# The first attention's second sequence: rows turned by VectorE and moved by DMA instead of turned by TensorE

## The chip, the cores and the metric

One core of a Trainium2 chip runs the whole kernel. Its engines are TensorE (matrix products, which it writes to PSUM), VectorE, ScalarE and GpSimd (called DVE, ACT and POOL in the profile), and SyncE (SP), which here only issues transfers; sixteen DMA engines carry what SP, ScalarE and GpSimd issue. Every engine works through its own list of instructions in order and waits at semaphores for the others. The metric is the device time of one execution in microseconds, the median of several runs.

## The reference, cut to what matters

Two transformer layers with a layer norm after each part. The change lies in the first part, a linear attention that reads a memory `M`, `z`:

```python
# L0_attn: B, S, HID = 2, 512, 512; H, HKV, D = 32, 8, 128; G = 4
q = (hidden_states @ Wq.T + bq).reshape(b, s, H, D)
sig_q = jax.nn.elu(q) + 1.0
q_sel = sig_q[:, :, ::G, :]                      # 8 heads are read
num = jnp.einsum('bshd,hde->bshe', q_sel, M)
den = jnp.einsum('bshd,hd->bsh', q_sel, z)[..., None] + EPS
retrieved = num / den
out_heads = jnp.repeat(retrieved, G, axis=2)
output = out_heads.reshape(b, s, H * D) @ Wo.T
...
x = _layernorm(x + _L0_attn_ref(x, ...))
x = _layernorm(x + _L0_ffn_ref(x, ...))
x = _layernorm(x + _L1_attn_ref(x, ...))
x = _layernorm(x + _L1_ffn_ref(x, ...))
```

The query product contracts over the 512 hidden columns, so each sequence's rows are needed with the hidden index on the partitions: the input has to be transposed.

## The kernel before

All arithmetic here is in float32. A sequence has 512 rows in four tiles `xs[b][t]` of 128 rows (on partitions) by 512 columns. `xt` is a sequence transposed: hidden index on partitions, four blocks `k` of 128, and 512 row positions in the free dimension. For each of eight heads `queries(b, xt, h)` makes four products into one PSUM tile `pq` (eight PSUM buffers in rotation), ScalarE takes Exp (L388) and Relu (L390) of it with the bias `bq`, and VectorE joins them to `q = min(e, 1) + r` (L392, called elu here). The tiles of `e` and `r` have two buffers, so the Exp of a head waits for the elu of two heads before. The sixteen `q` tiles are kept for the read stage.

The rows of sequence 0 are transposed tile by tile between products (`first_rows`, `first_queries`). Those of sequence 1 are transposed in one go after head 6 of sequence 0, by `transposed(xs[1], "a01")`: sixteen TensorE transposes into four PSUM tiles (L127), two copied out by ScalarE and two by VectorE (L129).

Meanwhile the weights are prepared. `sum_weights(eng, h)` adds up the four groups of `Wo` of a head (L407, L409; heads 1, 2, 4 and 6 on VectorE, 0, 3, 5 and 7 on GpSimd) from the tiles `wo`, a pool of six buffers, two to a head, so that a later head's load waits for an earlier head's sum; the result `wos` has four buffers. `turn_memory` transposes `M`. `fold(h)` multiplies the two (L414) and ScalarE writes the result with its row mean taken off to `mw[:, h, :511]` (L416, L417). The last column of `mw`, index `LAST`, holds `z`, copied by GpSimd at the start (L348). The first two folds come after head 0 of sequence 1, the others between later heads.

Beside that, the first feed-forward's weights are examined: `largest` reduces the first `gu` tile on VectorE, `over_partitions` (L190 to L194) and `scales` (L201 to L205) take the maximum over partitions by way of TensorE, and `check_up` then scales a block of `gu` on ScalarE (L463) and compares it on VectorE (L210). From head 3 of sequence 1 on there are three checks a head.

The read stage follows: for each of eight row tiles `read` multiplies the eight heads' `q` with `mw` (L428), ScalarE copies the denominators (L432) and scales three heads (L441), VectorE adds five (L450) and GpSimd the rest.

The loads are all issued by SP (but one row tile of sequence 0, by ScalarE) in this order: rows of sequence 0 and `wq` mixed, `wq` to the last, rows of sequence 1 (`load_x(1)`), `m`, the sixteen `wo` halves with the first `gu` before the last four, the other `gu`, then the second layer's small weights.

The order on each engine other than GpSimd is made by a planner that follows the program's order and its own estimate of when things are ready; `tc.issue_after(ins)` keeps what is traced inside it behind `ins` on that engine. GpSimd's list is in program order.

A later stage turns rows in another way already: `turn_squares` has VectorE transpose a tile in squares of 32 by 32 (L551), and `move_squares` moves the squares to their places with sixteen DMAs of 64 KB, 128 bytes a piece, on three queues (L292).

Of the kernel before, what the change touches and what calls it, by code (L numbers as in the profile page):

```python
# [10 lines left out]
F32 = mybir.dt.float32  # L11
# [3 lines left out]
AF = mybir.ActivationFunctionType  # L15
ALU = mybir.AluOpType
# [3 lines left out]
P = 128  # L20
B, S, HID = 2, 512, 512
NT = S // P
NK = HID // P
# [6 lines left out]
LAST = HID - 1  # L30
SQ = 32
# [7 lines left out]
def kernel(  # L39
# [19 lines left out]
    nc = tc.nc  # L59
# [6 lines left out]
    xtp = ctx.enter_context(tc.tile_pool(name="xtp", bufs=2))  # L66
# [14 lines left out]
    def psum(name):  # L81
        return ps.tile([P, 512], F32, tag="mm", name=name)


    xs = [[], []]

    def load_x(b, tiles=range(NT)):
        for t in tiles:
            x = xp.tile([P, HID], F32, tag="x", name=f"x_{b}_{t}")
            eng = nc.scalar if b == 0 and t == 1 else nc.sync  # L90
            eng.dma_start(x, x_in[b, ts(t, P), :])
            xs[b].append(x)

    load_x(0, range(2))
    bq = const.tile([D, NH], F32, tag="bq", name="bq")
    z = const.tile([D, NH], F32, tag="z", name="z")
# [18 lines left out]
    copies = []  # L115

    def transposed(rows, name, in_turn=False):

        xt = xtp.tile([P, NK, S], F32, tag="xt", name=f"xt_{name}")
        done = None  # L120
        for k in range(NK):
            pt = psum(f"pt_{name}_{k}")
            with ExitStack() as tied:
                if in_turn and k:
                    tied.enter_context(tc.issue_after(done.ins))
                for t in range(NT):
                    done = nc.tensor.transpose(pt[:, ts(t, P)], rows[t][:, ts(k, P)], ident)  # L127
            move = nc.vector.tensor_copy if k == 1 or k % 2 > in_turn else nc.scalar.copy
            copies.append(move(xt[:, k, :], pt))  # L129
        return xt  # L130
# [47 lines left out]
    def largest(blocks, name):  # L178

        k = len(blocks)  # L180
        mx = small.tile([P, k], F32, tag=f"mx{k}", name=f"mx_{name}", bufs=1)
        for i, w in enumerate(blocks):
            nc.vector.reduce_max(mx[:, i : i + 1], w, AX.X)
        return mx

    def over_partitions(mx, name):

        k = mx.shape[-1]
        pm = psum(f"pmx_{name}")
        nc.tensor.transpose(pm[:k, :P], mx, ident)  # L190
        top = small.tile([k, 1], F32, tag=f"top{k}", name=f"top_{name}", bufs=1)
        nc.vector.reduce_max(top, pm[:k, :P], AX.X)
        dg = small.tile([k, k], F32, tag=f"dg{k}", name=f"dg_{name}", bufs=1)
        nc.vector.tensor_scalar_mul(dg, ident[:k, :k], top)  # L194
        return dg
# [112 lines left out]
    with tc.tile_pool(name="a0w", bufs=1) as a0w, tc.tile_pool(name="a0", bufs=2) as a0:  # L308
        wq = []
        for h in range(NH):  # L310
# [7 lines left out]
            elif h == 1:  # L318
                nc.sync.dma_start(bq, bq_in)
                nc.sync.dma_start(z, z_in)  # L320
        load_x(1)
        m = a0w.tile([D, NH, D], F32, tag="m", name="m")
        nc.sync.dma_start(m, m_in)

# [20 lines left out]


        mw = a0w.tile([D, NH, HID], F32, tag="mw", name="mw")
        nc.gpsimd.tensor_copy(mw[:, :, LAST], z)  # L348

        def query_products(pq, xt, h, at):  # L350
            for k in range(NK):
                done = nc.tensor.matmul(  # L352
                    pq[:, at], wq[h][:, k, :], xt[:, k, at],
                    start=(k == 0), stop=(k == NK - 1),
                )
            return done

        def first_rows(xt, t):

            pt = psum(f"pt_a00_{t}")  # L360
            for k in range(NK):
                done = nc.tensor.transpose(pt[:, ts(k, P)], xs[0][t][:, ts(k, P)], ident)
            pt = pt.rearrange("p (k t) -> p k t", k=NK)
            nc.scalar.copy(xt[:, :2, ts(t, P)], pt[:, :2])
            nc.vector.tensor_copy(xt[:, 2:, ts(t, P)], pt[:, 2:])
            return done

        def first_queries(pq, xt):

            done = first_rows(xt, 0)  # L370
            for t in range(NT):
                if t + 1 < NT:
                    with tc.issue_after(done.ins):
                        done = first_rows(xt, t + 1)
                with tc.issue_after(done.ins):
                    done = query_products(pq, xt, 0, ts(t, P))
            return done

        def queries(b, xt, h):

            pq = psum(f"pq_{b}_{h}")
            if b == h == 0:
                done = first_queries(pq, xt)
            else:
                done = query_products(pq, xt, h, slice(0, S))

            e = a0.tile([D, S], F32, tag="e", name=f"e_{b}_{h}")
            nc.scalar.activation(e, pq, AF.Exp, bias=bq[:, h : h + 1])  # L388
            r = a0.tile([D, S], F32, tag="r", name=f"r_{b}_{h}")
            nc.scalar.activation(r, pq, AF.Relu, bias=bq[:, h : h + 1])  # L390
            q = a0.tile([D, S], F32, tag="q", name=f"q_{b}_{h}", bufs=16)
            nc.vector.scalar_tensor_tensor(q, e, 1.0, r, ALU.min, ALU.add)  # L392
            qs[b].append(q)
            return done

        def turn_memory():

            for i in range(2):
                pt = psum(f"pt_m_{i}")
                for j in range(4):  # L400
                    nc.tensor.transpose(pt[:, ts(j, P)], m[:, 4 * i + j, :], ident)
                nc.scalar.copy(m[:, 4 * i : 4 * i + 4, :].rearrange("d h e -> d (h e)"), pt)

        def sum_weights(eng, h):

            w, w1 = wos[h]
            eng.tensor_add(w, w, w1)  # L407
            s = a0.tile([D, HID], F32, tag="wos", name=f"wos{h}", bufs=4)
            eng.tensor_add(s, w[:, 0, :], w[:, 1, :])  # L409
            wos[h] = s  # L410

        def fold(h):
            p = psum(f"pmw_{h}")
            nc.tensor.matmul(p, m[:, h, :], wos[h], start=True, stop=True)  # L414
            c = small.tile([P, 1], F32, tag="col", name=f"col_{h}", bufs=2)
            nc.scalar.mul(c, p[:, LAST:], -1.0)  # L416
            nc.scalar.activation(mw[:, h, :LAST], p[:, :LAST], AF.Identity, bias=c)  # L417
# [65 lines left out]
        xt = xtp.tile([P, NK, S], F32, tag="xt", name="xt_a00")  # L483
        with tc.issue_after(queries(0, xt, 0).ins):
            queries(0, xt, 1)
        for h in range(2, NH):
            queries(0, xt, h)
            if h == 4:
                sum_weights(nc.gpsimd, 0)
                turn_memory()  # L490
                sum_weights(nc.vector, 1)
            elif h == 6:
                xt1 = transposed(xs[1], "a01")
                sum_weights(nc.vector, 2)
        sum_weights(nc.gpsimd, 3)
        for h in range(NH):
            queries(1, xt1, h)
            if h == 0:
                sum_weights(nc.vector, 4)
                sum_weights(nc.gpsimd, 5)  # L500
                fold(0)
                fold(1)
                with tc.issue_after(copies[-1].ins):
                    mx_up = largest(
                        [gus[0][:, a].rearrange("p k i -> p (k i)") for a in range(2)], "up"
                    )
            elif h == 1:
                top_up = over_partitions(mx_up, "up")
            elif h == 2:
                sc_up, inv_up = scales(top_up, "up")  # L510
                fold(2)
                fold(3)
                sum_weights(nc.vector, 6)
                sum_weights(nc.gpsimd, 7)
            elif h == 3:
                fold(4)
            elif h == 5:
                fold(5)
                fold(6)
            elif h == 6:  # L520
                fold(7)
            if h >= 3:
                for _ in range(3):
                    check_up(*checks.pop(0))
# [64 lines left out]
    xt1 = fp.tile([P, NT, NK, P], F32, tag="it11", name="xt_f01", bufs=1)  # L589
# [289 lines left out]
    for b in range(B):  # L879
# [5 lines left out]
        xt = xt_a1[b]  # L885
# [4 lines left out]
        for j in range(2):  # L890
            p = psum(f"pqk_{b}_{j}")
# [11 lines left out]
        for t in range(NT):  # L903
            p = psum(f"pv_{b}_{t}")
# [167 lines left out]
    t = NT - 1  # L1072
# [248 lines left out]
```

## Time and profile before

| | |
|---|---|
| median of three runs | 470.58 us (470.02 to 470.64) |
| the profiled execution | 470.72 us, span 468.7 us |
| granted TensorE clock, mean | 0.998 |
| TensorE, VectorE, ScalarE, GpSimd busy | 461.0, 329.5, 267.5, 115.1 us |
| query products (L352), 152 instructions | 56.9 us |
| folds and reads: first L428 product | starts at 72.32 us |

A time of the profile's lines counts from the start of the span. Sequence 0's heads run from about 6 to 37 us, sequence 1's to 72, the read stage to about 131; the feed-forward, the second attention and the second feed-forward take the rest, with TensorE busy throughout. A timeline line gives start, duration, engine, line, operation, output and inputs, shapes and count, and in brackets the idle time before it and what ended that. Lines of stretches give the length, the busy time of each engine with its number of instructions, the granted clock, the busy share of the DMA engines and GB/s.

### The profile page before, as it was taken

Reading aid. Unit: us, or ns where it says so; the run is one execution under the profiler, and the core shown is the slowest. Engines: PE = TensorE matmul, PEld = TensorE weight load, DVE = VectorE, ACT = ScalarE, POOL = GpSimd, SP = SyncE. Lnnn points to the kernel's source line nnn. Section 1 sums busy time; section 2 is a strip of 40 time slices with the busy share of each in tenths; the row PEclk is TensorE's granted clock in tenths of the full one; section 3 lists DMA queues with packets and bytes.
Section 4 is the critical chain, followed back from the end, with each engine's and each line's share of the span. In section 5 each row is a group of like instructions: output and inputs, shape, how many; then the busy total and the mean of one; then the engine's idle time right before and its main releaser. Section 6 shows DMA issues by size and latency. Waiting matters only on the chain.

```text
span 468.7 us, 5727 instructions
## 1 busy us (share of the span) xinstructions
PE 461.0 (98%) x1883; PEld 329.0 (70%) x1883; DVE 329.5 (70%) x627; ACT 267.5 (57%) x507; POOL 115.1 (25%) x144
## 2 busy tenths in 40 slices
PE   9999999999999999999999999999999999999994
PEld 8454444434478888888866567888888888888884
DVE  1165677767876767775979889895755778998632
ACT  3344799557756767456756842584645768443101
POOL 0235101566543053600357032000000000050111
PEclk9999999999999999999999999999999999999999
DMA  8989900000006500051390000000000000001001
GB/s 284 381 297 363 387 9 0 0 0 3 1 1 134 201 1 3 11 162 45 91 390 31 0 1 1 1 0 1 1 0 1 0 1 1 1 24 45 37 31 45
DMA packets 21651, 35.02 MB, mean 75 GB/s; under 512 B 9840, under 2 KB 10736, under 8 KB 21616
## 3 DMA queue, kind: packets, MB, share of 16 engines
q1 hardware_dynamic: 19616, 33.73, 20.7%
q10 hardware_dynamic: 1872, 0.56, 0.5%
q8 instruction: 22, 0.36, 0.3%
q0 software_dynamic: 128, 0.26, 0.3%
q14 instruction: 13, 0.11, 0.1%
HBM read 31.40 MB, written 2.10 MB: 71 GB/s over the span
## 4 chain that ended last, share of the span: by engine, by line
PE 71%; ACT 7%; DVE 5%; issue 3%; POOL 0%; POOLq 0%; DVEq 0%; ACTq 0%
PE pm L1111 17%; PE pg_f L611 9%; PE pu_f L611 9%; PE pc L1111 8%; PE pdm L1199 7%; PE pd_f L666 4%; PE pdc L1199 4%; DVE x L450 3%; PE pqk L893 3%; PE po L428 2%; ACT y L441 2%; ACT t L463 2%; PE pv L906 2%; PE pot L989 1%; PE po L1005 1%
## 5 line engine op out<-in xcount | busy, mean ns | idle before, releaser
L428 PE MATMUL po<-mw,q 128*128 128x512 f32 x128 | 57.1, 598 | 0.3 <-DVE mv_a L139 0.2
L352 PE MATMUL pq<-xt_a,wq 128*128 128x512 f32 (+1 forms) x152 | 56.9, 526 | 0.0
L145 POOL TENSOR_TENSOR rstd_f<-mv_f,ln_eps 128x1 f32<-128x1 f32 x15 | 4.4, 293 | 169.3 <-DVE mv_f L1214 130.2
L428 PEld LDWEIGHTS po<-mw,q 128*128 128x128 f32 x128 | 22.9, 189 | 32.1 <-issue 17.7
L352 PEld LDWEIGHTS pq<-xt_a,wq 128*128 128x128 f32 x152 | 26.2, 190 | 27.4 <-issue 25.7
L1111 PE MATMUL pm<-r,ugu 128*128 128x512 f32 x152 | 37.7, 389 | 0.0
L1111 PE MATMUL pm<-r,it_early 128*128 128x512 f32 x144 | 36.7, 392 | 0.0
L1111 PEld LDWEIGHTS pm<-r,ugu 128*128 128x128 f32 x152 | 28.5, 188 | 5.9
L1111 PEld LDWEIGHTS pm<-r,it_early 128*128 128x128 f32 x144 | 27.0, 188 | 6.1 <-issue 0.5
L169 ACT ACTIVATE ta_f<-y_f,below_half 128x512 int8<-128x512 f32 (+1 forms) x22 | 15.9, 721 | 27.0 <-DVE y_f L157 26.7
L450 DVE SCALAR_TENSOR_TENSOR x<-po,den,x 128x511 f32<-128x511 f32 x40 | 29.8, 745 | 1.9
L1121 DVE SCALAR_TENSOR_TENSOR ev_q<-pm,ev_q 128x512 f32<-128x512 f32 x27 | 18.6, 688 | 14.4 <-PE pm L1111 14.4
L637 DVE SCALAR_TENSOR_TENSOR it_f<-tb_f,ta_f 128x512 fp32r<-128x512 int16 (+1 forms) x22 | 15.4, 702 | 18.3 <-ACT tb_f L170 18.3
L445 POOL TENSOR_TENSOR y<-y,y 128x511 f32<-128x511 f32 x16 | 20.3, 1271 | 31.5 <-ACT y L441 30.8
L388 ACT ACTIVATE e<-pq,bq 128x512 f32<-128x512 f32 x16 | 11.1, 692 | 24.1 <-PE pq L352 20.6
L611 PE MATMUL pg_f<-xh,tu 128*128 128x512 f32 x88 | 24.3, 398 | 0.0
L1120 ACT ACTIVATE ev_q<-pc 128x512 f32<-128x512 f32 x27 | 16.0, 593 | 14.2 <-PE pc L1111 14.1
L465 POOL TENSOR_SCALAR td<-wd,inv_down 128x512 fp32r<-128x512 f32 x11 | 18.2, 1668 | 22.1 <-DVE inv_down L205 22.1
L611 PE MATMUL pg_f<-xl,tu 128*128 128x512 f32 x88 | 23.6, 390 | 0.0
L611 PE MATMUL pu_f<-xh,tu 128*128 128x512 f32 x88 | 23.5, 389 | 0.0
L611 PE MATMUL pu_f<-xl,tu 128*128 128x512 f32 x88 | 23.5, 389 | 0.0
L1001 ACT ACTIVATE x<-x,off_f,rstd_f 128x512 f32<-128x512 f32 x7 | 5.7, 816 | 27.7 <-POOL off_f L1000 27.7
(315 smaller groups left out, 1087.5 us busy)
## 6 DMA issues: line engine op xcount, KB each, us to landing
gu<-in_gu SPq DMA_DIRECT2D x20, 512.0 KB, 7.9
wo<-in_wo SPq DMA_DIRECT2D x16, 512.0 KB, 6.9
wd<-in_wd SPq DMA_DIRECT2D x20, 256.0 KB, 4.5
wq<-in_wq SPq DMA_DIRECT2D x8, 256.0 KB, 4.9
x<-in_x SPq DMA_DIRECT2D x7, 256.0 KB, 5.4
out<-x SPq DMA_DIRECT2D x7, 256.0 KB, 2.0
wqkv<-in_wqkv SPq DMA_DIRECT2D x1, 768.0 KB, 10.8
xt_f<-squares SPq DMA_DIRECT2D x9, 64.0 KB, 2.4
```

The lines of the kernel that those rows point to most:

```text
L169: nc.scalar.activation(a[:n], y, AF.Relu, bias=below_half[:n])
L352: done = nc.tensor.matmul(pq[:, at], wq[h][:, k, :], xt[:, k, at], start=(k == 0), stop=(k == NK - 1),)
L428: nc.tensor.matmul(po, qs[b][h0 + j][:, ts(t, P)], mw[:, h0 + j, :], start=True, stop=True,)
L445: nc.gpsimd.tensor_add(ys[0][:, :LAST], ys[0][:, :LAST], y[:, :LAST])
L450: steps.append(nc.vector.scalar_tensor_tensor(x[:, :LAST], four[j][:, :LAST], d, x[:, :LAST], ALU.mult, ALU.add))
L465: eng.tensor_scalar(out, w, factor, None, ALU.mult)
L611: nc.tensor.matmul(pp[a], t[:, a, i % NK, :], x2[b][i], start=(i == 0), stop=(i == 2 * NK - 1),)
L666: nc.tensor.matmul(pd, inter[b][c][:, ts(t, P)], td[c].bitcast(F32R), start=(c == 0), stop=(c == last),)
L1111: nc.tensor.matmul(p, w, x, start=(left[id(p)] == begun[id(p)]), stop=(left[id(p)] == 1))
L1120: nc.scalar.activation(ev, pc, AF.Copy, scale=CROSS)
L1121: nc.vector.scalar_tensor_tensor(ev, pm, MAIN, ev, ALU.mult, ALU.add)
L1199: nc.tensor.matmul(p[:, :w], got[j // 4][1][kind][:, j % 4], down_parts[j][kind][:, cols], start=(j == 0 and kind == kinds[0]), stop=(j == ...
```

## The change

Sequence 1's rows are no longer transposed by TensorE. VectorE transposes each row tile in squares of 32 by 32 into `turned_rows`, a part of `mw` that is not yet in use, so laid out that 128 row positions with the same place in their square lie side by side. Sixteen DMAs on ScalarE's queue then move strips of 32 partitions, in pieces of 512 bytes, to `xt1`: `move_rows(i)` issues four, for row positions `i*128` to `i*128+127`. Two groups of eight are issued, behind the Relu of head 0 and that of head 1. The row positions of `xt1` are in another order than the rows; Exp and Relu of sequence 1 write their results in the right order by a rearranged output (`ordered`).

The loads of sequence 1's rows are issued after `wq2`, ahead of `wq3` to `wq7`. The copy of `z` into the last column of `mw` comes after sequence 1's first head in the program. Three orders are tied anew: the turns behind the last copy of `first_rows`, the third head's sum behind the fourth elu, and the `gu` maximum behind the seventh elu (before: behind the last copy of `transposed`).

```diff
             elif h == 1:
                 nc.sync.dma_start(bq, bq_in)
                 nc.sync.dma_start(z, z_in)
-        load_x(1)
+            elif h == 2:
+                load_x(1)
...
         mw = a0w.tile([D, NH, HID], F32, tag="mw", name="mw")
-        nc.gpsimd.tensor_copy(mw[:, :, LAST], z)
-
...
+        turned_rows = mw[:, :NT, :].rearrange("p a f -> p (a f)")
+        turned_rows = turned_rows.rearrange("p (b t c) -> p b t c", t=NT, c=SQ)
+        xt1 = xtp.tile([P, NK, S], F32, tag="xt", name="xt_a01")
+
+        def turn_rows(t):
+            nc.vector.transpose(
+                turned_rows[:, :, t, :], xs[1][t].rearrange("p (b c) -> p b c", c=SQ)
+            )
+
+        def move_rows(i):
+
+            src = mw[:, :NT, :].rearrange("p a f -> p (a f)")
+            src = src.rearrange("p (k j f) -> p k j f", k=NK, j=P // SQ)
+            for j in range(P // SQ):
+                nc.scalar.dma_start(xt1[ts(j, SQ), :, ts(i, P)], src[ts(i, SQ), :, j, :])
+
...
-            nc.vector.tensor_copy(xt[:, 2:, ts(t, P)], pt[:, 2:])
+            copies.append(nc.vector.tensor_copy(xt[:, 2:, ts(t, P)], pt[:, 2:]))
             return done
...
+        relus, elus = [], []
+
         def queries(b, xt, h):
...
             e = a0.tile([D, S], F32, tag="e", name=f"e_{b}_{h}")
-            nc.scalar.activation(e, pq, AF.Exp, bias=bq[:, h : h + 1])
+
+            if b == 1:
+                pq = pq.rearrange("p (i t c) -> p i t c", t=NT, c=SQ)
+
+            def ordered(u):
+                return u.rearrange("p (t i c) -> p i t c", t=NT, c=SQ) if b == 1 else u
+
+            nc.scalar.activation(ordered(e), pq, AF.Exp, bias=bq[:, h : h + 1])
             r = a0.tile([D, S], F32, tag="r", name=f"r_{b}_{h}")
-            nc.scalar.activation(r, pq, AF.Relu, bias=bq[:, h : h + 1])
+            relus.append(nc.scalar.activation(ordered(r), pq, AF.Relu, bias=bq[:, h : h + 1]))
             q = a0.tile([D, S], F32, tag="q", name=f"q_{b}_{h}", bufs=16)
-            nc.vector.scalar_tensor_tensor(q, e, 1.0, r, ALU.min, ALU.add)
+            elus.append(nc.vector.scalar_tensor_tensor(q, e, 1.0, r, ALU.min, ALU.add))
...
         with tc.issue_after(queries(0, xt, 0).ins):
             queries(0, xt, 1)
+        with tc.issue_after(copies[-1].ins):
+            for t in range(NT):
+                turn_rows(t)
         for h in range(2, NH):
+            with tc.issue_after(relus[h - 2].ins):
+                if h < 4:
+                    for i in range(2):
+                        move_rows(2 * h - 4 + i)
             queries(0, xt, h)
             if h == 4:
                 sum_weights(nc.gpsimd, 0)
                 turn_memory()
                 sum_weights(nc.vector, 1)
             elif h == 6:
-                xt1 = transposed(xs[1], "a01")
-                sum_weights(nc.vector, 2)
+                with tc.issue_after(elus[3].ins):
+                    sum_weights(nc.vector, 2)
         sum_weights(nc.gpsimd, 3)
         for h in range(NH):
             queries(1, xt1, h)
             if h == 0:
+                nc.gpsimd.tensor_copy(mw[:, :, LAST], z)
                 sum_weights(nc.vector, 4)
...
-                with tc.issue_after(copies[-1].ins):
+                with tc.issue_after(elus[6].ins):
                     mx_up = largest(
```

## The prediction

> **What bounds the kernel now.** I read the page first, then the chain of waits, then each engine's timeline over the first 75 us, then the stretch table. The page says TensorE is busy 98% of the span; the stretches show where that holds for the stage of the change:
>
> ```profile
> core 0: us, PE busy (x) PEld busy (x) DVE busy (x) ACT busy (x) POOL busy (x), PEclk, DMA share, GB/s
> 0.00:11.70 11.70, 10.65 (x67) 9.95 (x68) 1.90 (x9) 3.56 (x7) 0.92 (x8) 1.00 0.85 283
> 11.70:23.40 11.70, 11.70 (x29) 5.19 (x28) 1.78 (x3) 4.27 (x7) 2.84 (x2) 1.00 1.00 382
> 23.40:32.00 8.60, 8.60 (x27) 4.20 (x26) 6.00 (x7) 3.49 (x6) 3.27 (x3) 1.00 0.83 266
> 32.00:40.00 8.00, 8.00 (x32) 4.46 (x31) 5.07 (x8) 3.49 (x6) 3.76 (x2) 1.00 0.99 386
> 40.00:51.00 11.00, 11.00 (x29) 4.86 (x28) 4.47 (x9) 5.29 (x10) 3.77 (x2) 1.00 0.98 374
> 51.00:60.00 9.00, 9.00 (x23) 3.98 (x22) 7.36 (x14) 8.38 (x17) 1.45 (x1) 1.00 0.86 320
> 60.00:72.00 12.00, 12.00 (x30) 5.30 (x29) 8.68 (x22) 12.00 (x24) 0.00 (x0) 1.00 0.01 2
> ```
>
> From 11.7 to 51 us TensorE has no gap, at full clock, while ScalarE and VectorE are busy under half of most of these stretches: TensorE sets the pace. The DMA engines are full too (share 0.83 to 1.00), which matters below. From 51 to 72 ScalarE is full beside TensorE. The timeline of TensorE shows the work that the change removes (start, duration, line, tile, count):
>
> ```profile
> 25.32 7.03 PE L352 MATMUL pq<-xt_a,wq 128*128 128x512 f32 x16
> 32.19 1.91 PE L127 MATMUL pt_a<-ident,x 128*128 128x128 f32 x16
> 33.94 7.03 PE L352 MATMUL pq<-xt_a,wq 128*128 128x512 f32 x16
> ```
>
> The products resume at 33.94, so the 16 transposes hold the array for 33.94 - 32.19 = 1.75 us. Of the 7.03 us that follow the first half is head 7 of sequence 0; head 0 of sequence 1 begins at 33.94 + 3.43 = 37.37 (3.43 is the step from one head to the next), the first reader of the turned rows.
>
> **Part by part.** *Removed*: 1.75 us of TensorE, on the path. Also two ScalarE copies (1.07 us at 33.54) and two VectorE copies (2 x 0.68 at 35.11 and 36.31); both engines have idle time there, so nothing. Sum so far -1.75.
>
> *Loads moved on SP's queue.* The four row loads (1 MB) pass five wq loads, wq3 to wq7, and the latter come four issues later. So wq3 takes the place of wq7, issued 8.2 and landed 4.8 us later, at 13.0; head 3 starts at 17.8. Cover 4.8 us, growing by about 2 us a head: nothing. Later loads keep their place. The row loads take the places of wq3 to wq6, the last issued about 7.5 with 4.1 to landing: rows there at 11.6.
>
> *Added on VectorE*: four square transposes. The same instruction on the same shape is in the trace:
>
> ```profile
> 122.08 0.71 DVE L551 STREAM_TRANSPOSE squares<-x 128x512 f32<-128x512 f32 x1
> 141.19 2.10 ACTq L292 DMA_DIRECT2D xt_f<-squares  x3
> ```
>
> 4 x 0.71 = 2.84 us. VectorE is idle 2.25 us before 12.21, 2.74 before 15.64 and 6.67 before 23.00, so they fit; the last ends at 11.6 + 0.71 = 12.3 at best, 13.5 if the first elu (12.21, 0.69) goes ahead. I take 13.
>
> *Added on ScalarE's queue*: 16 issues. Bounds of one: 0.42 us (the row load of 128 pieces on this queue at 0.74) and 0.70 (the three above, 512 pieces each). The new ones have 128 pieces, so I take 0.42: 6.7 us, at most 11.2. Behind them wait the Exp and Relu of heads 1 and 2, and behind those VectorE's elu and two of the eight PSUM buffers. ScalarE's idle time between 12.2 and 32.4 is 12.9 us, and no head's result is read before the read stage at 72: nothing, unless ScalarE falls some 13 us behind (four heads of 3.43 us in the buffers, an estimate). First group 13.0 to 16.4, head 1's Exp and Relu 1.25, second group to 21.0 (25.5 by the upper price).
>
> *When the rows have landed.* The 64 KB moves here took 2.2 to 3.9 us on this queue with no load beside them; loads in the busy stretch took up to 9.5. So 23.2 to 35.0. They are wanted at 37.37 - 1.75 = 35.62. Even the upper end is in time. One rule of the skill speaks against this: "DMA: Bandwidth & Descriptors", section "Rules for kernel authors", calls transfers under 64 KB mostly overhead, and the page's fit in "Anatomy of one DMA", for GpSimd's path, makes 2.15 us of each. One after another that is 34 us, by estimate, and rows at 47: TensorE would wait 11.8 us, 480.8 in all. The trace overlaps them: sixteen such moves, issued from 141.19 on over three queues, had landed by 150.3, 9.1 us.
>
> *The DMA engines carry 1 MB more.* Bounds: 1.05 MB at the 400 GB/s of the best microseconds (16 to 23) is 2.6 us; the 128-byte moves of 141 to 150 took 0.69 x 9 = 6.2. Pieces of 512 bytes lie between; I take 3. Loads behind it (wo, then gu) come so much later, less some 1.5 us of idle share between 23 and 30. Who is late next: VectorE, which stands in order behind a load:
>
> ```profile
> 33.37 1.22 DVE L407 TENSOR_TENSOR wo<-wo,wo 128x1024 f32<-128x1024 f32 x1 [3.97 <-DMA wo<-in_wo]
> ...
> 39.84 1.23 DVE L407 TENSOR_TENSOR wo<-wo,wo 128x1024 f32<-128x1024 f32 x1 [1.45 <-DMA wo<-in_wo]
> 40.98 0.68 DVE L392 SCALAR_TENSOR_TENSOR q<-e,r 128x512 f32<-128x512 f32 x1
> 41.86 0.69 DVE L409 TENSOR_TENSOR wos<-wo 128x512 f32<-128x512 f32 x1 [0.20 <-PE pmw L414]
> 42.47 0.69 DVE L392 SCALAR_TENSOR_TENSOR q<-e,r 128x512 f32<-128x512 f32 x1
> 46.26 0.28 DVE L192 TENSOR_REDUCE top_up<-pmx_up 2x1 f32<-2x128 f32 x1 [3.11 <-PE pmx_up L190]
> ```
>
> If the load at 39.84 is d later, the work behind it ends at 42.9 + d (the small wait for pmw gone), and top_up with dg_up at 43.4 + d. TensorE wants dg_up at 49.59 - 1.75 = 47.84 (pbc_up, L201). So d up to 4.4 costs nothing; by my bounds d is at most 6.2 - 1.5 = 4.7, a wait of 0.3 at most. The first gu load lands at 37.1 + d and feeds pmx_up at 45.95 - 1.75 = 44.2 after a reduce of 1.28: cover 5.8. The second (39.0 + 7.4 = 46.4) is wanted on ScalarE at 54.08 - 1.75: cover 5.9.
>
> *z's column copy* (0.20 us on GpSimd) moves behind the landing of the moves and ahead of a sum that began at 35.97 and whose result goes into a buffer free only at 42.83: nothing. The fold that writes the same tile comes at 42.36: later than the moves.
>
> *Exp and Relu with reordered writes* (16, runs of 32). No row has such runs. The nearest is L364, 256 elements in two runs, 0.372 us against 0.585 for 512 in one: the slope of 0.83 ns leaves 0.16, the whole of a one-column instruction (L416, 0.17), so a break in a run costs at most 0.01 us. 15 breaks x 0.01 x the ten in ScalarE's full stretch (heads 3 to 7) = 1.5 us as the upper end; I take nothing, as the two runs cost nothing.
>
> *Does the gain pass the ScalarE-bound stretch?* That stretch starts on TensorE's word (inv_up at 50.2 after pbc_up), so it starts 1.75 earlier with the same work in it. Sum: 470.72 (the profiled execution, span 468.7) - 1.75 = 468.97; the median of the runs is 0.14 lower: **468.8**.
>
> **Rivals.**
> *1. The two queues share their places in flight (slower).* SP's issues wait for older landings (in the view of waits: who, for what, us in total, times, longest):
>
> ```profile
> SPq L332 <- DMA wo<-in_wo: 5.6, 2, 4.8
> SPq L314 <- DMA x<-in_x: 1.7, 2, 1.4
> ```
>
> and the wq load issued about 6.8 goes out as the row load eight issues before it lands (1.64 + 5.2). If ScalarE's moves draw on the same eight places, the eighth move waits for wo2's last half (issued 15.5, landed 25), the second group goes out 26.3 to 29.7 and the third head's wo load, free to go at 22.8, waits until about 29: 6.2 late, some 8 with the added megabyte. The rows still land before 35.6. But d = 8 is 3.6 over the 4.4 above: TensorE waits 3.6 at L201, net +1.85, **472.4**. It decides from d = 4.4 and turns the sign at 6.2. For it: the waits shown. Against: only SP issues here, so sharing is not seen, and the planner may place VectorE's blocked sum elsewhere.
> *2. The gain is eaten in ScalarE's full stretch (no change).* 12.00 of 12.00 busy from 60 to 72: with reordered writes at their upper end, 1.5 of the 1.75 is lost, **470.3**. Against: the L364 row. A planner's new order of that stretch could do the same.
> *3. Rows late.* If moves and loads share the engines packet by packet, loads of 2 to 4 KB against 512 bytes, the last may land after 37.37. At 41, **474.2**. Against: the 35.0 bound above.
>
> **How the numbers follow.** A difference under 0.2% (0.94 us) can't be told from no change. Forecast 0.54, own range 468.0 to 469.6 (1.75 less up to 0.8 lost, more by up to 0.8 if a shift of VectorE's order also closes small waits in the read stage, where TensorE has 80 products in 35.47 against 34.3 at the head's pace). Rival 2: 0.17, within 0.2%. Rival 1: 0.20, rival 3: 0.09, slower. The range 468.0 to 472.8 takes in rival 1 and leaves out the high end.
>
> **What would show it.** Right: no transposes between heads 6 and 7; the first product of sequence 1 near 35.6 with no gap before it; pbc_up near 47.8; ScalarE's den column at 73.0 in place of 74.79; Exp of sequence 1 at 0.69. Wrong: a gap of TensorE before the first pq of sequence 1 (rival 3); a gap before pbc_up with VectorE held by a wo load, and ScalarE's issues spread out to 25 us or more (rival 1); Exp and Relu above 0.8 us (rival 2).

## The result, and the profile after

The changed kernel takes **472.69 us** (median of 15 runs, 470.67 to 474.13) against 470.64 (470.02 to 471.16) for the kernel before on the same chip: ratio 1.0044, 95% interval 1.0032 to 1.0055. It is slower by 2.05 us, where 1.8 less was forecast. The profiled execution took 473.49 (span 471.7), 2.77 more than the one of before and 0.8 above its own median; the steps below are read from it. Of all executions in this document one, of e8_half, took 795.71 us at a mean granted clock of 0.557; it is left out of that run's figures.

TensorE's timeline first (start, duration, line, tile, count, and in brackets the idle time ahead and what ended it):

```profile
25.13 10.46 PE L351 MATMUL pq<-xt_a,wq 128*128 128x512 f32 x24
38.68 5.12 PE L351 MATMUL pq<-xt_a,wq 128*128 128x512 f32 x8 [3.08 <-ACT m L427]
43.64 1.88 PE L439 MATMUL pmw<-wos,m 128*128 128x512 f32 x4
45.35 3.60 PE L351 MATMUL pq<-xt_a,wq 128*128 128x512 f32 x8
...
52.42 0.38 PE L201 MATMUL pbc_up<-dg_up,ones 2*128 2x2 f32 x2
```

Before, head 1 of sequence 1 began here:

```profile
42.52 3.60 PE L352 MATMUL pq<-xt_a,wq 128*128 128x512 f32 x8
```

The transposes between head 7 of sequence 0 and head 0 of sequence 1 are gone, and sequence 0 ends at 35.59; 35.62 was forecast. But then TensorE stands still for 3.08 us, so that the first head of sequence 1 starts at 38.68 instead of 37.37 before: 1.31 later. The same eight products that take 3.60 one head later take 5.12 here: 1.52 more. Together 2.83, which is 45.35 less the 42.52 at which the next head began before. It is passed on whole: the read stage begins at 75.15 (72.32 before), and the span is 3.0 longer. The stretches show the second term (length, then busy time and instructions of TensorE, its weight loads, VectorE, ScalarE and GpSimd, then granted clock, DMA share and GB/s):

```profile
36.00:37.00 1.00, 0.00 (x0) 0.00 (x0) 0.00 (x0) 1.00 (x3) 0.57 (x1) 1.00 0.87 215
...
38.00:39.00 1.00, 0.32 (x1) 0.35 (x2) 1.00 (x3) 0.65 (x2) 0.42 (x1) 0.60 0.88 307
39.00:40.00 1.00, 1.00 (x2) 0.48 (x2) 1.00 (x2) 0.85 (x2) 0.11 (x1) 0.50 1.01 410
40.00:41.00 1.00, 1.00 (x2) 0.34 (x2) 1.00 (x3) 0.53 (x2) 0.00 (x0) 0.50 0.99 332
41.00:42.00 1.00, 1.00 (x3) 0.39 (x2) 0.99 (x2) 1.00 (x2) 0.00 (x0) 0.70 0.75 225
42.00:43.00 1.00, 1.00 (x4) 0.49 (x3) 0.82 (x2) 1.00 (x3) 0.82 (x1) 1.00 0.83 143
```

After the wait the granted clock is 0.5 to 0.7 for some 3 us. From 36 to 37 TensorE and VectorE are idle, GpSimd for nearly half, and ScalarE is full: it is catching up. Why it is behind shows in its own timeline, with its DMA issues (ACTq):

```profile
12.48 3.15 ACTq L372 DMA_DIRECT2D xt_a<-mw  x3
15.68 0.69 ACT L413 ACTIVATE e<-pq,bq 128x512 f32<-128x512 f32 x1 [3.69 <-DMA wq<-in_wq]
16.27 0.68 ACT L415 ACTIVATE r<-pq,bq 128x512 f32<-128x512 f32 x1
16.93 8.63 ACTq L372 DMA_DIRECT2D xt_a<-mw  x5
25.67 0.69 ACT L413 ACTIVATE e<-pq,bq 128x512 f32<-128x512 f32 x1 [8.72 <-DMA xt_a<-mw]
...
27.00 8.17 ACTq L372 DMA_DIRECT2D xt_a<-mw  x8
35.27 0.69 ACT L413 ACTIVATE e<-pq,bq 128x512 f32<-128x512 f32 x1 [8.33 <-DMA xt_a<-mw]
...
37.56 1.09 ACT L427 COPY m<-pt_m 128x512 f32<-128x512 f32 x2
```

The Exp of head 3 stood here before:

```profile
21.21 0.69 ACT L388 ACTIVATE e<-pq,bq 128x512 f32<-128x512 f32 x1 [2.17 <-PE pq L352]
```

It runs at 35.27 now, 14 us late. One issue takes 0.59 us, so five are 2.95, yet they need 8.63: the rest is waiting for earlier transfers to land. The trace's semaphore records show which. A transfer tells its landing by a semaphore; SP's and ScalarE's transfers take turns on the same eight, and an issue waits until the last user of its semaphore has landed. Of the last eight moves five go out 0.02 us after such a landing (at 27.00, 29.15, 30.83, 33.09 and 34.57); three of the five ahead of them wait in the same way for loads of SP (`m` and two of `wo`). In e1, where GpSimd issues the moves, they use eight others. So the "places in flight" of the prediction are semaphores of this program.

What TensorE waited for at 38.68 is not what the bracket says. The copies of the turned M end at 38.65 (37.56 + 1.09), and the profile puts the wait down to them, because they came last. But the last move, issued at 34.57, landed at 38.33, and that is near too. GpSimd's copy of `z`, which may run only when the moves have read `mw`, began 0.10 us before TensorE:

```profile
38.58 0.53 POOL L531 COPY mw<-z 128x8 f32<-128x8 f32 x1 [2.00 <-DVE wo L432]
```

Two other profiles with the same wait part the two: e12, the changed kernel once more, and e7 (below). First e12, then e7:

```profile
36.80 1.09 ACT L427 COPY m<-pt_m 128x512 f32<-128x512 f32 x2
38.46 0.24 POOL L531 COPY mw<-z 128x8 f32<-128x8 f32 x1 [3.39 <-DMA xt_a<-mw]
38.56 5.20 PE L351 MATMUL pq<-xt_a,wq 128*128 128x512 f32 x8 [3.48 <-ACT e L413]
```

```profile
36.91 1.09 ACT L429 COPY m<-pt_m 128x512 f32<-128x512 f32 x2
37.67 0.27 POOL L533 COPY mw<-z 128x8 f32<-128x8 f32 x1 [1.76 <-DMA xt_a<-mw]
37.77 5.37 PE L353 MATMUL pq<-xt_a,wq 128*128 128x512 f32 x8 [2.50 <-ACT m L429]
```

TensorE starts 0.10 us after the copy of `z` and 0.34 or 0.35 after the landing of the last move (38.33, 38.22 in e12, 37.42 in e7) in all three. The copies of M end 0.03 us before TensorE starts, 0.67 before it (e12) and 0.23 after it (e7). So the rows set its start; the copies, and the PSUM buffers that they free, did not.

In the view of waits (who, for what, us in total, times, longest) both queues wait for the moves:

```profile
ACT e L413 <- DMA xt_a<-mw: 17.1, 2, 8.7
...
SPq L333 <- DMA xt_a<-mw: 7.5, 3, 3.9
```

(The wait put down to the Exp is that of the issues ahead of it.) SP's loads of `wo` wait for ScalarE's moves. And VectorE, in order, waits behind those loads:

```profile
37.23 1.23 DVE L432 TENSOR_TENSOR wo<-wo,wo 128x1024 f32<-128x1024 f32 x1 [9.56 <-DMA wo<-in_wo]
...
46.85 1.23 DVE L432 TENSOR_TENSOR wo<-wo,wo 128x1024 f32<-128x1024 f32 x1 [2.79 <-DMA wo<-in_wo]
...
50.11 0.22 DVE L194 TENSOR_SCALAR dg_up<-ident,top_up 2x2 f32<-2x2 f32 x1
```

Head 6's sum is at 46.85 (39.84 before): the delay called d in the prediction is **7.0 us**, not 3. It costs nothing here, as dg_up is still 2.1 us ahead of pbc_up at 52.42. But pbc_up is late itself: without the wait at the first head it would be wanted near 47.8.

### The profile page after: what moved, and what is told of

The parts are those of the page before. It is cut to its first block, busy times and chain, and to the rows that moved or that the text cites. A ratio compares the mean times of both kernels' runs of the same rounds, so it can differ in the third digit from the quotient of the medians.

```text
span 471.7 us, 5725 instructions
## 1 busy us (share of the span) xinstructions
PE 460.5 (98%) x1867; PEld 327.1 (69%) x1867; DVE 329.9 (70%) x629; ACT 266.6 (57%) x505; POOL 115.7 (25%) x144
## 4 chain that ended last, share of the span: by engine, by line
PE 79%; ACT 5%; issue 2%; DVE 0%; POOL 0%; POOLq 0%
PE pm L1144 17%; PE po L453 10%; PE pg_f L644 9%; PE pu_f L644 8%; PE pc L1144 8%; PE pdm L1232 7%; PE pd_f L699 4%; PE pdc L1232 4%; PE pqk L926 3%; ACT t L488 2%; PE pv L939 2%; PE pot L1022 1%; PE po L1038 1%; PE psc L964 1%; ACT tu L488 1%
## 5 line engine op out<-in xcount | busy, mean ns | idle before, releaser
L351 PE MATMUL pq<-xt_a,wq 128*128 128x512 f32 (+1 forms) x152 | 58.5, 537 | 3.1 <-ACT m L427 3.1
```

Of the source, the lines that this page charges most:

```text
L351: done = nc.tensor.matmul(pq[:, at], wq[h][:, k, :], xt[:, k, at], start=(k == 0), stop=(k == NK - 1),)
```

## The experiments

Ratios are to the kernel before, run on the same chip beside them.

**e1_pool: the moves issued by GpSimd.**

```diff
-                nc.scalar.dma_start(xt1[ts(j, SQ), :, ts(i, P)], src[ts(i, SQ), :, j, :])
+                nc.gpsimd.dma_start(xt1[ts(j, SQ), :, ts(i, P)], src[ts(i, SQ), :, j, :])
```

> The sixteen moves go out on GpSimd's queue, all else as in the changed kernel. Theory A (ScalarE's issues and SP's loads share eight places in flight, each issue waits for an older landing, and ScalarE stands still meanwhile): GpSimd's transfers have places of their own, sixteen issues of 0.65 us from 12.4 are out by 23, ScalarE's Exp follow TensorE again, the rows have landed by 30 to 34, before the 35.6 at which they are wanted, no gap in TensorE: 468.9, 0.4 either way. Theory B (the DMA engines themselves are too full for another megabyte): landing takes 6 to 10 us a move whatever the queue, the last one still lands near 38, TensorE waits some 2 to 3 us: 471.5 or more.

474.6 against 470.91, ratio 1.0077 [1.0058, 1.0097]; profiled 473.32. TensorE's and VectorE's timelines:

```profile
24.74 13.90 PE L351 MATMUL pq<-xt_a,wq 128*128 128x512 f32 x32
...
50.00 0.35 PE L201 MATMUL pbc_up<-dg_up,ones 2*128 2x2 f32 x2 [2.61 <-DVE dg_up L194]
...
81.88 8.40 PE L453 MATMUL po<-mw,q 128*128 128x512 f32 x15 [2.15 <-ACT y L466]
```

```profile
46.38 1.22 DVE L432 TENSOR_TENSOR wo<-wo,wo 128x1024 f32<-128x1024 f32 x1 [2.84 <-DMA wo<-in_wo]
```

The 32 products from 24.74 on run into sequence 1 with no gap: with ScalarE free, the rows are in time. But the loads stay 6.5 us late though the moves have a queue of their own, and the wait moves to pbc_up (2.61) and on into the read stage (2.15, with a granted clock of 0.50 from 83 to 86 us). The Trainium skill's "DMA: Bandwidth & Descriptors", section "Issuing engines are not separate DMA queues", says that transfers run on the same 16 engines whichever engine starts them; this run agrees. Its addition, that another issuer saves only issuing time, holds for the loads (6.5 late against 7.0) but not for the issuer: the 14 us by which ScalarE was late, and with them the first wait, are gone.

**e2_seq0: no turns and no moves; sequence 1's queries read sequence 0's rows.** All other parts of the change stay.

```diff
-            for t in range(NT):
-                turn_rows(t)
...
-                    for i in range(2):
-                        move_rows(2 * h - 4 + i)
...
-            queries(1, xt1, h)
+            queries(1, xt, h)
```

> Leaves out the turning and moving of sequence 1's rows: its queries read the transposed rows of sequence 0. Load order, reordered writes of Exp and Relu, z's copy and the ties stay. It is the ceiling of the change. If the reordered writes and the load order cost nothing and the gain passes the stretch in which ScalarE is full, 470.6 - 1.75 = 468.9. If the gain is eaten there (rival 2 of the prediction), 470.3.

469.33 against 470.91, ratio 0.9961 [0.9949, 0.9974]. TensorE's timeline:

```profile
25.32 13.90 PE L351 MATMUL pq<-xt_a,wq 128*128 128x512 f32 x32
...
47.85 0.38 PE L201 MATMUL pbc_up<-dg_up,ones 2*128 2x2 f32 x2
```

pbc_up comes at 47.85, where 47.84 was forecast, the read stage at 70.58 instead of 72.32, and 1.6 of the 1.75 us reach the end. The saving is real and passes ScalarE's full stretch; what eats it is in the turns or the moves.

**e4_pe_rows: the other parts alone.** TensorE turns the rows as before; the order of the loads, the late copy of z and the new order of VectorE's work are those of the change.

```diff
-                    for i in range(2):
-                        move_rows(2 * h - 4 + i)
...
+                xt1 = transposed(xs[1], "a01")
```

> TensorE transposes sequence 1's rows as before and Exp and Relu write in order, while the earlier load of the rows, the later copy of z and the new ties stay: the change without its core. All theories: 470.6, within 0.4, if these parts cost nothing. 471.5 or more would put part of the loss on the load order.

470.78 against 470.91, ratio 0.9995 [0.9986, 1.0004]. These parts cost nothing.

**e3_fill: head 7's products computed twice, to give TensorE work in place of the wait.**

```diff
+                if b == 0 and h == NH - 1:
+                    done = query_products(pq, xt, h, slice(0, S))
```

> The changed kernel with head 7 of sequence 0 multiplied twice: 3.43 us more work for TensorE just where it waited 3.08 us. Theory C (1.5 of the lost microseconds are the halved clock after the wait, seen as 5.12 us for two heads' worth of records that take 3.60): the clock stays full, sequence 1's first head takes 3.43 and the kernel is about 1.1 us faster than the changed one, 471.6, though it does more. If the wait alone costs and the clock doesn't, 0.35 us slower than the changed one, 473.0.

473.84 against 470.91, ratio 1.0071 [1.0054, 1.0088]. TensorE's timeline:

```profile
25.27 17.33 PE L351 MATMUL pq<-xt_a,wq 128*128 128x512 f32 x40
...
44.15 3.60 PE L351 MATMUL pq<-xt_a,wq 128*128 128x512 f32 x8
...
51.78 0.35 PE L201 MATMUL pbc_up<-dg_up,ones 2*128 2x2 f32 x2 [0.49 <-DVE dg_up L194]
```

With 3.43 us of useless work, the second head of sequence 1 starts at 44.15, earlier than the 45.35 of the change: no wait, and the clock is 1.00 in every microsecond from 36 to 43. So the 1.52 us are the price of the lowered clock, not of slow operands. In total it is no faster: pbc_up waits for VectorE, and the read stage gains 0.7 (74.48). The whole kernel doesn't show even this. A wait of TensorE of 0.75 us at 231 to 236 us, behind GpSimd's rstd, is in the profiles of e2, e3 and e4 and not in those of the two main kernels; it isn't explained.

**e6_unread: all moves on ScalarE's queue as in the change, read by nobody** (sequence 1's queries read sequence 0's rows).

```diff
-            queries(1, xt1, h)
+            queries(1, xt, h)
```

> Leaves out the use of the moved rows: turns and moves run as in the changed kernel, but sequence 1's queries read sequence 0's transposed rows, so that nothing waits for a landing. Theory A1 (ScalarE held at its issues till 35 is enough: Exp, Relu and the copies of M come late and no PSUM buffer is free): the gap of about 3 us before sequence 1's first head stays, 472.4. Theory A2 (what TensorE waits for is the landing of the last rows, the PSUM buffer only comes near it): no gap or under 1 us there, 470.0 or less.

472.43 against 470.69, ratio 1.0038 [1.0019, 1.0057]: 3.1 above e2 by the medians and 3.6 by the ratios, with the same products. Moving the megabyte costs this much even if no product waits for it. TensorE's timeline:

```profile
25.77 13.90 PE L351 MATMUL pq<-xt_a,wq 128*128 128x512 f32 x32
...
50.71 0.35 PE L201 MATMUL pbc_up<-dg_up,ones 2*128 2x2 f32 x2 [2.34 <-DVE dg_up L194]
50.99 3.31 PE L439 MATMUL pmw<-wos,m 128*128 128x512 f32 x4
```

There is no wait at the first head, but one of 2.34 at pbc_up, with the clock at 0.5 after it (four folds in 3.31 instead of 1.98). Most of it isn't the late load: head 6's sum is 5.5 us late (45.30), 1.1 over the 4.4, but dg_up itself took 2.00 us instead of 0.22, beside a weight sum of GpSimd. In this execution ScalarE's last issue ended at 32.0, 3 us earlier than in the change, so that neither theory A1 nor A2 would have had TensorE wait long at the first head: the run alone doesn't decide between them.

**e5_pool_tie and e7_tie: head 6's sum placed behind dg_up,** in e1 and in the changed kernel.

```diff
+                with tc.issue_after(spread["up"].ins):
-                sum_weights(nc.vector, 6)
+                    sum_weights(nc.vector, 6)
```

> Moves on GpSimd's queue as in the first experiment, and VectorE's sum of head 6's weights (which stood before top_up and waited for its load until 46.4) tied behind dg_up. Theory D (with the moves off ScalarE the only wait left in the stage is TensorE's 2.6 us at pbc_up, behind that load): pbc_up at 47.4, no gap of TensorE before the read stage, 469.3, 0.6 either way, faster than both kernels. If the later loads or ScalarE's late checks hold the read stage anyway, as in the 2.15 us gap at 79.7 of the first experiment: 471 to 473.

> The changed kernel with head 6's sum tied behind dg_up and nothing else. All theories: the late load at VectorE is hidden behind the wait at sequence 1's first head (dg_up done 2.1 us before pbc_up there), so the time stays that of the changed kernel, 472.7, 0.6 either way. 471.5 or less would make the late load the main cause.

e5: 472.96 against 470.69, ratio 1.0049 [1.0031, 1.0067]; 469.3 was hoped for. With head 6's sum out of the way there is a wait of 0.77 at pmx_up (behind head 4's sum, itself 7.1 us behind its load), one of 0.86 at pbc_up and one of 2.31 in the read stage. e7: 471.73, ratio 1.0036 [1.0009, 1.0062], below the 472.1 that was expected at least, but too wide to part from the change; in its profile the first head waits 2.50, the next eight products take 5.37, and pbc_up doesn't wait. In e5 the wait that is taken away is replaced by the next ones behind the same late loads.

**e8_half and e9_half_pool: half of the moves.** Rows 0 to 63 of each tile go by VectorE and DMA (8 moves, 0.5 MB, the first group); TensorE transposes rows 64 to 127. In e9 GpSimd issues the moves.

```diff
-                if h < 4:
+                if h < 3:
                     for i in range(2):
                         move_rows(2 * h - 4 + i)
...
             elif h == 6:
+                half_rows()
...
+                        nc.tensor.transpose(
+                            pt[:, ts(4 * k + t, 2 * SQ)],
+                            xs[1][t][2 * SQ :, ts(2 * u + k, P)], ident[2 * SQ :, 2 * SQ :],
+                        )
```

> Half the moves: only rows 0 to 63 of each tile go by VectorE and ScalarE's queue (8 moves, 0.5 MB); TensorE transposes rows 64 to 127 of each tile between heads 6 and 7 of sequence 0, 16 transposes of 64 columns, so at most 0.87 of the 1.75 us can be saved. Theory F (delay in proportion to the bytes: head 6's sum 3.5 us late instead of 7.0, under the 4.4 us from which pbc_up waits; ScalarE free of issues by about 26, rows landed by 32): no wait at sequence 1's first head, none at pbc_up, 469.8, ratio 0.998. Theory G (the shared places set the delay, whatever the bytes, or the first eight moves are the costly ones): d of 4.4 or more, a wait at pbc_up above 0.5 us, 470.6 or more, ratio 1.000 or above.

> As e8_half, with the eight moves issued by GpSimd. Theory F: d about 3.3 (half of the 6.5 with all sixteen on that queue), ScalarE free throughout, no wait at the first head or at pbc_up: 469.8, ratio 0.998. Theory H (GpSimd's issues delay its weight sums and its sums slow VectorE, and that is what made the waits of the sixteen, more than the bytes): waits at pbc_up or in the read stage of 0.5 us or more in all though d is under 4.4: 470.5 or more.

e8's profile took 469.65, and TensorE and VectorE show:

```profile
31.93 1.21 PE L380 MATMUL pt_a<-ident,x 64*128 64x64 f32 x16
33.08 7.13 PE L351 MATMUL pq<-xt_a,wq 128*128 128x512 f32 x16
...
48.84 0.38 PE L201 MATMUL pbc_up<-dg_up,ones 2*128 2x2 f32 x2
```

```profile
40.01 1.23 DVE L449 TENSOR_TENSOR wo<-wo,wo 128x1024 f32<-128x1024 f32 x1 [1.87 <-DMA wo<-in_wo]
```

The sixteen half transposes hold the array for 33.08 - 31.93 = 1.15 us, 0.60 less than the whole ones, no product waits, and head 6's sum is 0.2 us late, not half of 7.0. SP still waits 5.4 us in all for ScalarE's moves here, so the shared semaphores don't make the loads late. The DMA queues between 10 and 50 us say part of why (queue, packets, MB, the time of its packets as a share of 16 engines; q1 is SP's, q10 ScalarE's). Before:

```profile
q1 hardware_dynamic: 4211, 13.98, 95.2%
```

After:

```profile
q1 hardware_dynamic: 3418, 11.13, 85.1%
q10 hardware_dynamic: 2304, 1.05, 10.7%
```

With half of the moves:

```profile
q1 hardware_dynamic: 4174, 13.89, 95.2%
q10 hardware_dynamic: 1152, 0.52, 5.1%
```

Before, the engines were idle for 4.7% of these 40 us, 1.9 us; half of the moves take 5.1%, 2.0 us, and just fit. All of them take 4.3 us, and the loads get slower too: 11.13 MB in 34.0 us (85.1% of 40) is 0.327 MB a us, against 13.98 in 38.1, 0.367; at that rate they would have needed 30.3, so 3.7 us are lost. 4.3 + 3.7 = 8.0, and the measured delay is 7.0. This is an account of the delay, not its cause. The other profiles repeat it: 0.327 to 0.348 with all moves, whoever issues them (e1, e3, e5, e6, e7, e12), 0.361 to 0.365 with half of them, 0.370 and 0.375 in e2 and e4. But the loads stay slower from 38.5 to 50 us, when no move is in flight any more; before, then after:

```profile
q1 hardware_dynamic: 1141, 4.16, 96.3%
```

```profile
q1 hardware_dynamic: 971, 3.54, 89.0%
```

That is 4.16 MB in 11.07 us, 0.376 a us, against 3.54 in 10.24, 0.346. So moves in flight beside them can't be the whole reason; what makes the loads slower isn't shown.

As a version e8 isn't established: eleven of its executions fall into two groups, 469.3 to 470.26 (six) and 472.4 to 475.19 (five); ratio 1.0025 [0.9999, 1.0051]. e9: 473.03, ratio 1.0053 [1.0029, 1.0077]; its profile, at 471.35, has head 6's sum 1.8 late (41.60), no wait up to the read stage, and still no gain. Neither theory explains that, but the trace shows where it went. Heads 5 to 7 of sequence 0 began 0.27 us later than before, and the products ahead of and behind the transposes took 0.32 longer, which is all of the 0.6 saved, so that the read stage begins at 72.30 (72.32 before); the feed-forward begins level too (130.62 and 130.65), and 1.4 us are lost in it, at 153 to 156 us, where TensorE waits for casts by ScalarE (L278). Why these come late there isn't shown.

**e10_half_again, e11_half_third, e12_after_again: two more profiles of e8 and one more of the change.**

> e8_half unchanged, profiled once more: eleven of its executions fall into two groups, six between 469.3 and 470.3 and five between 472.4 and 475.2, and its one profile is of the first group (469.65, no wait of TensorE in the stage). If the moves' landing decides which group an execution falls into, a profile above 472 shows head 6's sum some 3 us or more later than the 40.01 of the first and TensorE waiting at the first head of sequence 1, at pbc_up or in the read stage. If the second group comes from elsewhere, the stage up to 75 us is as in the first profile and the time is lost later. A profile of the first group again says nothing.

> As e10_half_again: a third profile of the same kernel, to have one of each group with a chance of some three in four.

> The changed kernel unchanged, profiled once more: its executions lie between 470.67 and 474.13 and its profile was at 473.49. If the spread comes from when the moves land, a profile under 472 shows ScalarE's issues ending before 33 and a wait at sequence 1's first head under 1 us, and one near 473 the same 2.5 to 3.1 us at that place.

e8 took 469.68 and 469.33 beside 470.70 for the kernel before, again with no wait and head 6's sum at 39.30 and 40.41. All three profiles are of the lower group, so where the upper one loses its 3 to 5 us was not seen. The change took 473.51, and TensorE the same path:

```profile
38.56 5.20 PE L351 MATMUL pq<-xt_a,wq 128*128 128x512 f32 x8 [3.48 <-ACT e L413]
```

Here the copies of M had ended at 37.9, 0.7 ahead, and the last move landed at 38.22 (see above): the rows held TensorE, though the bracket names ScalarE.

What the executions have in common: the kernels without moves spread over 0.8 to 1.9 us (e2, e4, and before, but for one of its executions at 473.07), those with moves over 2.5 to 6.2. If the moves land at another time in each execution, the wait differs with it; this would fit, but no trace of a long one of e8 shows it.

## Why the prediction was wrong

The direction was wrong; the place of the gain was right. Point by point:

- **TensorE saves 1.75 us: right.** It is free at 35.59 (forecast 35.62; its products had begun 0.19 earlier, at 25.13 and not 25.32), and e2 brings 1.6 of it to the end. That rules out rival 2 as well: sequence 1's Exp and Relu with reordered writes take 0.69 and 0.68, e4 leaves the rest of the change at 0.9995, and the gain passes the stretch in which ScalarE is full.
- **The turns on VectorE: right.** Four in 2.65 us from 9.68 to 12.3, hidden. The moved wq loads and z's copy: nothing on TensorE's path.
- **The price of the issues, "6.7 us, at most 11.2", and with it "Even the upper end is in time": the step that failed.** One issue at 0.59 lies inside the bounds of 0.42 and 0.70; but the sum took the sixteen to go out one behind the other, and each waits for the transfer that used its semaphore last. The planner put three behind head 0's Relu, five behind head 1's and eight behind head 2's. They were put at 13.0 to 16.4 and at most to 25.5, and ran from 12.48 to 25.56 and 27.00 to 35.17. So the last rows, forecast for 23.2 to 35.0 and wanted at 35.62, landed at 38.33, and TensorE stood for 3.08 us. The shared places in flight, which would have given this, were left to rival 1 because the trace of before has one issuer only. The time in flight, 3.8 to 10.0 us, was near the 9.5 of the upper end; that end only started from an issue at 25.5. The moves did overlap: rows at 47, by one after another, were not seen.
- **"nothing, unless ScalarE falls some 13 us behind": the condition was met, its consequence not seen.** ScalarE fell 14 us behind, but in the three profiles with the wait TensorE waited for the rows and not for a PSUM buffer.
- **d, the delay of the later loads: 3 taken, 4.7 at most, 7.0 measured.** The moves' own time (4.3 of engine time, bounds 2.6 to 6.2) was inside; that the loads get a tenth slower was not in the sum. The 4.4 us from which d costs was tested by e1: with d at 6.5 the wait at pbc_up is 2.61, where 6.5 - 4.4 = 2.1 follows from the prediction, and TensorE's products had begun 0.58 earlier there (24.74).
- **The price of a wait: too low.** The prediction adds the idle time alone; a wait of 3.08 cost 4.6 in all, with the halved clock after it.
- **The rivals.** Rival 1 (472.4) comes nearest to the 472.69, with its mechanism of shared places, which SP's waits for ScalarE's moves show. But it had the rows in time and the wait at pbc_up. The wait came at rival 3's place, the first head, for rival 3's reason, late rows, and by rival 1's cause; that the number is rival 1's is in part luck. pbc_up is where e1 and e6 wait. In e1 the moves have a queue and semaphores of their own and the loads are late all the same, and in e8 SP waits 5.4 us for the moves and the loads are in time: shared places explain ScalarE's hold and the late rows, not the 7 us of the loads. The range 468.0 to 472.8 held the time only through rival 1, and its 0.20 was too little: SP's waits on landings were in the trace, and eight further issues in front of them had no cover but an estimate.

**What is settled and what is open.** Settled: the moves eat the gain and more (e2, e4, e6); on ScalarE's queue the rows come late, since issues wait for landings, and on GpSimd's they don't (e1); the lowered clock after the wait costs another 1.5 us (e3). Neither GpSimd's queue nor a later place for head 6's sum nor both saved it (e1, e5, e7): with 1 MB more the loads themselves are late. Half of the moves delayed them by -0.5 to 0.6 us in three profiles of e8 and by 1.8 in e9. Open: why the loads are slower even when no move is in flight, why the moves make executions differ, and so whether half of them is a gain. No version that beats both kernels was established.

## What to carry to other kernels

Before moving work from an engine to DMA, read the DMA share of the very stretch: moves of 2.0 us beside 1.9 us of idle share caused no wait in three profiles (though five of eleven executions were 3 to 5 us slower), while twice as much went with loads 7 us late. An issue on an engine that has work in order behind it is priced by the landing of the transfers ahead of it, not by the issue: 0.59 us became 1.0 to 1.7 each, and the engine's whole lead went. Where two things end within 0.3 us of a wait's end, another profile can tell which one ended it. When loads are late, follow every consumer in order; taking away the first wait shows the next.

## What the runs showed of the hardware

**The clock falls after short waits, not always.** After TensorE stood for 3.08 us (the change), 3.48 (e12), 2.50 (e7), 2.34 (e6), and for 2.15 (e1) and 2.31 (e5) in the read stage, the granted clock was 0.5 to 0.7 for about 3 us; after 2.61 at pbc_up in e1 it stayed at 1.00. So the length alone doesn't decide. The Trainium skill, "TensorE: Matmul & The Clock Gate", Part 1, puts the fall after an idle window of some 3.4 us and calls the window free-running. Here waits of less than two thirds of that length are enough in some places, so a wait of over 2 us is better priced with up to 1.8 us more: the eight products behind it took 5.12, 5.20 and 5.37 us instead of 3.60.

**Neighbours slow small work.** dg_up, 2 x 2 elements, takes 0.22 us in the change and 2.01 in e3, where GpSimd's weight sum runs beside it.
